# Four graph-attention layers with a planned instruction order: the planner models the port that VectorE and GpSimd share, and work moves between VectorE, GpSimd and SyncE

## The chip, the cores and the metric

The kernel runs on one core of one Trainium2 chip. The metric is the device time of one execution in microseconds (us); lower is better. The engines are called PE (TensorE matmul), PEld (its weight load), DVE (VectorE), ACT (ScalarE), POOL (GpSimd) and SP (SyncE). SP computes nothing here; it issues DMAs.

## The reference

There are 128 graphs of 128 nodes with 512 float32 features each (`x`), and one 128 x 128 integer adjacency matrix per graph (`adj`). Four layers follow each other, each a graph attention, a residual and a layer norm:

```
x = layernorm(x + gat0(x, adj))   # scores x.w_src + x.w_dst + b; leaky relu; softmax over adj + eye; mixes x itself
x = layernorm(x + gat1(adj, x))   # x @ W1 (4 heads of 256), attention, elu, then @ W2 (1024 -> 512), attention
x = layernorm(x + gat2(x, adj))   # 8 heads of 64
x = layernorm(x + gat3(x, adj))   # scores through W_fc and W_attn, mixes x itself, elu
```

Each attention is softmax(leaky_relu(s[i] + t[j]), masked by the adjacency) times a feature matrix. Graphs don't depend on each other.

## The kernel before, in words

**Tiling.** One graph is one tile: its 128 nodes are the 128 partitions, its 512 features lie along the free dimension. Everything is float32. All weights stay in SBUF; each graph's `x` is loaded once and its result stored once; the adjacency is loaded twice.

**One graph's work.** `graph(g)` builds a list of operations. Each `Op` has an engine, a cost that the planner charges, and a function that emits its instructions.

- `first` (layer 0): loads `x` (L834) and the adjacency (L835). Builds the masks: the adjacency plus the identity (`ae`, L838) and then `mask` (L738), which turns integers into 0 or a large negative number. Two dot products with the score weights (`score`, L744). Then spread, attention, mixing, residual and norm.
- `spread`: puts a column of scores into a row on all partitions. VectorE transposes the column (L589), one DMA writes it to a row in DRAM (L592), and a second reads it back broadcast over 128 partitions (L596).
- `attend`: `prelu` on ACT (L646), the masked sum with its row extreme on VectorE (L654), `exp` on ACT (L663), the reciprocal on VectorE (L671), for two of the attentions a scaling on POOL (L673), then `turned`.
- `turned`: transposes a tile. VectorE transposes 32 x 32 blocks (L607), one DMA writes them to scratch DRAM (L612), and a second reads them back with the blocks in their new places (L617 or L622).
- `project` (L710, copies out L717) multiplies by W1 or by layer 2's weights; `mixed` (L725) and `heads` (L938) multiply attention by features; `block` (L896) does so for layer 1. `halves` (L794) multiplies by W2 for two graphs together with fewer products, for which POOL forms sums and differences of the operands (L780).
- `norm`: statistics (L681, L682) on VectorE, the root on ACT (L685, L686), the `offset` (L692, and L696 in layer 2) and the scaling on ACT (L699).
- `third` (layers 2 and 3): loads the adjacency again (L975), and ends with elu (L981, L982), a sum on POOL (L986), the norm and the store (L988).

**The order.** Nothing is ordered by hand. `Pipeline.plan` places one graph's operations in a repeating period of `PERIOD` us, each engine taken by one operation at a time; from these times come the events of all graphs and the number of slots of each buffer. `Pipeline.order` then walks through the events of all 128 graphs: among those no further than `AHEAD` us past the oldest one not yet issued, it issues what could start first, by its own modelled clock of each engine, of the DMA lane and of the buffers. It uses `FLOW` for the time from one operation to a reader. `SEED` and `SPREAD` set a random shift in `plan`'s priorities. What it yields is each engine's fixed instruction order; on the chip each engine runs its own order strictly, and semaphores hold it where data or a buffer isn't ready. The modelled times are not enforced.

The weights and their derived columns are prepared by the operations of the list `setup`, which carry times of their own, up to about 200 us into the plan. POOL has four weight loads and 33 operations there.

Of the kernel before, what the change touches and what calls it, by code (L numbers as in the profile page):

```python
# [14 lines left out]
ALU = mybir.AluOpType  # L15
# [14 lines left out]

PERIOD = 28.0
LATENCY = {"PE": (0.0, 0.8), "DVE": (0.15, 1.44), "ACT": (0.1, 1.44), "POOL": (0.1, 1.44), "SP": (7.06, 7.06)}
FLOW = {"PE": (0.0, 0.6), "DVE": (0.15, 0.8), "ACT": (0.1, 0.8), "POOL": (0.1, 0.8), "SP": (4.5, 4.5)}
AHEAD = 20.0
URGENCY = 0.6
BANKS = 8

SEED, SPREAD = 989, 8.0

# [21 lines left out]
class Op:  # L61
    def __init__(self, engine, cost, emit, ins, outs, extra, uses=(), dma=0.0):
        self.dma = dma
        self.engine, self.cost, self.emit, self.extra = engine, cost, emit, extra
        self.wait = 0
        self.ins, self.outs = ins, outs
        self.uses = list(uses)
        self.bufs = list(dict.fromkeys([*ins, *outs, *uses]))

    def done(self, reader=None):  # L70
        own, other = LATENCY[self.engine]
        return self.cost + self.extra + (own if reader is self.engine else other)


class Pipeline:
# [3 lines left out]
    def plan(self, ops):  # L79
# [23 lines left out]
        taken = {e: [] for e in LATENCY}  # L103
        times, ready, missing = [0.0] * len(ops), [0.0] * len(ops), [len(q) for q in before]
# [3 lines left out]
        while waiting:  # L108
            k = min(waiting, key=lambda k: (ready[k] - URGENCY * left[k] + shift[k], k))
            waiting.remove(k)  # L110
            op, t = ops[k], ready[k]
            spans = taken[op.engine]
            while True:
                u = t % PERIOD
                clash = [
                    y + d - u for x, y in spans for d in (-PERIOD, 0.0, PERIOD)
                    if u < y + d - 1e-9 and x + d < u + op.cost - 1e-9
                ]
                if not clash:
                    break  # L120
                t += min(clash) + 1e-9
                assert t < ready[k] + 2 * PERIOD, "the period is too short"
            spans.append((t % PERIOD, t % PERIOD + op.cost))
            times[k] = t
# [20 lines left out]
    def order(self, events):  # L145

        ops, n = [e[3] for e in events], len(events)
# [33 lines left out]
        known = {e: [i for i in range(n) if not before[i] and ops[i].engine == e] for e in FLOW}  # L181
        issued, low, out = [False] * n, 0, []

        def start(i):
            t = max(clock[ops[i].engine], ready[i])
            for b in makes[i]:

                rank = 0
                for q in coming[b.tag]:
                    if q >= i or rank >= len(free[b.tag]):  # L190
                        break
                    rank += 1
                if rank >= len(free[b.tag]):
                    return None
                t = max(t, free[b.tag][rank][0])
            return t

        while len(out) < n:
# [21 lines left out]
            clock[op.engine] = done = t + op.cost  # L220
            own, other = FLOW[op.engine]
            if op.engine == "POOL":
                other += op.extra
            if op.dma:

                done = lane = max(lane, done) + op.dma
                own = other = FLOW["SP"][0]
            for q in after[i]:
# [15 lines left out]
def tile_gat_stack(  # L244
# [322 lines left out]
    def graph(g):  # L567

        ops = []

        def op(engine, cost, emit, ins=(), outs=(), extra=0.0, uses=(), dma=0.0):
            ops.append(Op(engine, cost, emit, list(ins), list(outs), extra, uses, dma))

# [5 lines left out]

        def spread(col, nh):  # L580

# [3 lines left out]
            def turn():  # L585
# [5 lines left out]
            op("DVE", 0.12 + 0.033 * nh, turn, [col.buf], [sT])  # L591
            op("SP", 0.6, lambda: nc.sync.dma_start(  # L592
                out=row.ap.rearrange("h (b c) -> b h c", b=P // 32), in_=sT.ap[0:P:32]
            ), [sT], [row], dma=0.02 + 0.03 * nh)
            db = Buf(f"db{nh}", [P, nh, P])
            op("SP", 0.4, lambda: nc.sync.dma_start(  # L596
                out=db.ap.rearrange("p h j -> p (h j)"),
# [4 lines left out]
        def turned(src, n, moving=False):  # L602
# [8 lines left out]
            ), [src], [zb])  # L611
            op("SP", 0.4, lambda: nc.sync.dma_start(  # L612
                out=scr.ap, in_=zb.ap.rearrange("p b h c -> p (b h c)")
            ), [zb], [scr], 0.2 * n, dma=0.05 + 0.17 * n)
            flat = lambda: scr.ap.rearrange("p f -> (p f)")
            if moving:
                op("SP", 0.6, lambda: nc.sync.dma_start(  # L617
                    out=out.ap.rearrange("p h i -> p (h i)").rearrange("p (q e) -> p q e", q=4),
                    in_=flat().rearrange("(q p e) -> p q e", q=4, p=P),
                ), [scr], [out], 1.0, dma=0.27 + 0.15 * n)  # L620
                return out
            op("SP", 0.65, lambda: nc.sync.dma_start(  # L622
                out=out.ap.rearrange("p h (q c) -> p h q c", q=4),
# [13 lines left out]
        def attend(db, h0, nh, src, mask, scaled=False):  # L637
# [30 lines left out]
            op("ACT", 0.08 + 0.293 * nh, prelu, [db, src.buf], [z])  # L668
            op("DVE", 0.08 + 0.225 * nh, masked, [z, mask], [zz, nm])
            op("ACT", 0.39 * nh, exp, [zz, nm], [zz, rs])  # L670
            op("DVE", 0.07, lambda: nc.vector.reciprocal(ri.ap, rs.ap), [rs], [ri])  # L671
            if scaled:
                op("POOL", 0.15 + 0.29 * nh, lambda: nc.gpsimd.tensor_mul(  # L673
                    zz.ap, zz.ap, ri.ap.unsqueeze(2).to_broadcast([P, nh, P])
                ), [zz, ri], [zz])
            return turned(zz, nh, moving=scaled), ri

        def norm(y, plus=0.0):
# [12 lines left out]
            def offset():  # L691
                nc.gpsimd.tensor_scalar(  # L692
                    out=mr.ap, in0=mv.ap[:, 0:1], scalar1=rd.ap, scalar2=-1.0, op0=ALU.mult, op1=ALU.mult
                )
                if plus:
                    nc.gpsimd.tensor_scalar_add(mr.ap, mr.ap, plus)  # L696

            op("POOL", 0.6 if plus else 0.3, offset, [mv, rd], [mr])
            op("ACT", 0.7, lambda: nc.scalar.activation(  # L699
# [37 lines left out]
        def mask(m, a, what):  # L737
            op("POOL", 0.75, lambda: nc.gpsimd.tensor_scalar(  # L738
                out=m.ap, in0=a.ap, scalar1=0.0, scalar2=-BIG, op0=what, op1=ALU.mult
            ), [a], [m], 2.0)  # L740

        def score(xv, wv, init, sc, s):
# [3 lines left out]
                accum_out=sc.ap[:, s : s + 1],  # L746
            ), [xv], [jk, sc], uses=[*w0b, b0b])

# [115 lines left out]
        def second(g, st, xl):  # L864
# [15 lines left out]
            for nh in range(2):  # L880
                op("POOL", 1.3, lambda nh=nh: nc.gpsimd.tensor_add(  # L881
                    xl.ap[:, nh, : 2 * FH], xl.ap[:, nh, : 2 * FH], b1t[:, nh * 2 * FH : (nh + 1) * 2 * FH]
                ), [xl], [xl], uses=[b1b])
# [27 lines left out]
        def third(g, st, xl2):  # L911

            m1, m2, xb = (st[n] for n in ("m1", "m2", "xb"))
            sc2 = small("sc2", 2)
            op("DVE", 0.07, lambda: nc.vector.tensor_add(sc2.ap, xl2.ap[:, :, F // 2], shift2.ap), [xl2], [sc2], uses=[shift2])
            db = spread(Col(sc2, 0, 1), 1)
# [43 lines left out]

            op("DVE", 0.2, scores, [z3, xl3], [sc4])
            mv, rd = norm(x3, plus=1.0)
# [7 lines left out]

            op("DVE", 0.15, normed, [sc4, mv, rd], [sc4], uses=[swf])
# [79 lines left out]
```

## Time and profile before

| what | us |
|---|---|
| median of 3 runs | 3219.89 (3217.49 to 3227.5) |
| the profiled execution's own time | 3260.22 |
| its span, first to last instruction | 3258.4 |
| PE busy | 3066.8 |
| VectorE busy | 2779.0 |
| ACT busy | 2451.2 |
| POOL busy | 1895.1 |

How to read it: busy time is that of the profiled execution, and the share of the span alone does not say what bounds a stage. Time in which an instruction waits for a port counts as busy; time in which it waits for a semaphore counts as idle. DMA-issuing instructions on SP don't count as busy. `A <- B` after a wait names who waited and what released it. The granted PE clock is 0.976 on average: 1.00 in the steady part, less in the first 150 and the last 150 us.

### The profile page before, as it was taken

What the parts mean: (1) busy time and instruction counts of PE and PEld (TensorE: products, weight loads), DVE (VectorE), ACT (ScalarE), POOL (GpSimd) and SP (SyncE); (2) the same over time, 40 slices, a digit from 0 to 9 for tenths busy, and PEclk for the clock granted to TensorE, in tenths of its full rate; (3) what the DMA queues carried; (4) which work ended last, traced back from release to release, by engine and by line L of the source; (5) the groups of instructions that cost most, each with busy time, mean ns of one, the idle gap of its engine ahead of it and who ended that gap; (6) DMA issues with size and microseconds to landing.
All of it is one profiled execution on the core that took longest, in us unless ns stands there. A gap on an engine that the chain in (4) does not pass through costs nothing. (4 is left out here: it accounts for less than half of the span.)

```text
span 3258.4 us, 62058 instructions
## 1 busy us (share of the span) xinstructions
PE 3066.8 (94%) x14822; PEld 2488.7 (76%) x14822; DVE 2779.0 (85%) x9833; ACT 2451.2 (75%) x8741; POOL 1895.1 (58%) x2347
## 2 busy tenths in 40 slices
PE   6899999999999999999999999999999999999984
PEld 4688887787777877877777778777787777878853
DVE  4779888888888988898888889889898898989875
ACT  2457787787777777787777877777877777778875
POOL 4655655665565655665555665565566556565533
PEclk7899999999999999999999999999999999999985
DMA  4358777877877877877778777877787787777875
GB/s 119 94 136 196 183 205 188 200 193 190 203 187 188 205 186 192 201 190 200 188 187 200 191 188 204 189 190 201 191 204 187 188 205 188 196 196 190 197 174 129
DMA packets 1657567, 606.08 MB, mean 186 GB/s; under 512 B 1311562, under 2 KB 1508170, under 8 KB 1657204
## 3 DMA queue, kind: packets, MB, share of 16 engines
q1 hardware_dynamic: 1655836, 598.97, 75.0%
q8 instruction: 120, 1.97, 0.2%
q14 instruction: 243, 1.99, 0.2%
q0 software_dynamic: 576, 2.10, 0.2%
q10 hardware_dynamic: 792, 1.06, 0.1%
HBM read 374.43 MB, written 227.48 MB: 185 GB/s over the span
## 5 line engine op out<-in xcount | busy, mean ns | idle before, releaser
L710 PE MATMUL ps<-w1s,w 128*128 128x258 f32 x4096 | 926.9, 384 | 48.5 <-DMA w<-scr 25.0
L710 PEld LDWEIGHTS ps<-w1s,w 128*128 128x128 f32 x4096 | 777.0, 191 | 186.3 <-DVE xl L812 39.5
L654 DVE CUSTOM_DVE_ANT_0 w<-w,w 128x128 f32<-128x128 f32 x1920 | 861.1, 544 | 65.6 <-ACT w L646 49.2
L794 PE MATMUL ps<-w2s,w 128*128 128x257 f32 x3584 | 849.0, 383 | 8.5 <-POOL w L780 8.4
L663 ACT ACTIVATE w<-w,nm 128x128 f32<-128x128 f32 x1920 | 748.0, 394 | 98.2 <-DVE nm L654 76.3
L794 PEld LDWEIGHTS ps<-w2s,w 128*128 128x128 f32 x3584 | 669.1, 191 | 188.8 <-issue 80.0
L646 ACT ACTIVATE w<-w,xl 128x128 f32<-128x128 f32 x1536 | 488.8, 389 | 279.9 <-DMA w<-row 259.1
L607 DVE STREAM_TRANSPOSE w<-w 128x512 f32<-128x512 f32 (+1 forms) x1024 | 551.5, 540 | 34.3 <-ACT w L663 13.3
L710 PE MATMUL ps<-wha,w 128*128 128x273 f32 x2048 | 502.3, 398 | 7.3 <-DMA w<-scr 6.9
L710 PEld LDWEIGHTS ps<-wha,w 128*128 128x128 f32 x2048 | 383.2, 192 | 87.4 <-DVE w L607 6.3
L699 ACT ACTIVATE w<-w,mr,rd 128x512 f32<-128x512 f32 x512 | 415.2, 811 | 33.9 <-POOL mr L692 33.0
L692 POOL TENSOR_SCALAR mr<-mv,rd 128x1 f32<-128x1 f32 x512 | 160.1, 313 | 409.4 <-ACT rd L686 201.8
L663 ACT ACTIVATION_READ_ACCUMULATOR w<-w,nm 128x1 f32 x1920 | 368.1, 192 | 0.0
L681 DVE BATCH_NORM_STATS2 st<-w 128x6 f32<-128x512 f32 x512 | 337.2, 668 | 5.4 <-POOL w L986 4.6
L881 POOL TENSOR_TENSOR xl<-xl,b1t 128x512 f32<-128x512 f32 x256 | 335.2, 1310 | 1.6
L938 PEld LDWEIGHTS ps<-xl,w 128*128 128x128 f32 x2048 | 274.3, 196 | 80.8 <-issue 24.4
L646 ACT ACTIVATE w<-w,sc 128x128 f32<-128x128 f32 x384 | 152.3, 397 | 227.6 <-DMA w<-row 226.6
L725 PE MATMUL ps<-w,w 128*128 128x512 f32 x512 | 277.4, 624 | 32.6 <-DMA w<-scr 31.6
L738 POOL TENSOR_SCALAR w<-adj 128x128 f32<-128x128 int32 x256 | 192.4, 752 | 188.2 <-DMA adj<-in_adj_dram 75.1
L717 ACT COPY xl<-ps 128x258 f32<-128x258 f32 (+1 forms) x768 | 273.2, 362 | 31.8 <-PE ps L710 31.3
L938 PE MATMUL ps<-xl,w 128*128 128x66 f32 x2048 | 265.2, 273 | 27.7 <-DMA w<-scr 14.4
L654 DVE DVE_READ_ACCUMULATOR2_ANT nm<- 128x1 f32 x1920 | 290.5, 151 | 0.0
(213 smaller groups left out, 4258.8 us busy)
## 6 DMA issues: line engine op xcount, KB each, us to landing
scr<-w SPq DMA_DIRECT2D x640, 256.0 KB
w<-scr SPq DMA_DIRECT2D x640, 256.0 KB
w<-row SPq DMA_DIRECT2D x128, 512.0 KB
w<-in_x_dram SPq DMA_DIRECT2D x128, 256.0 KB
w<-row SPq DMA_DIRECT2D x128, 256.0 KB
out_dram<-w SPq DMA_DIRECT2D x128, 256.0 KB
w<-row SPq DMA_DIRECT2D x384, 64.0 KB
scr<-w SPq DMA_DIRECT2D x384, 64.0 KB
```

Of the source, the lines that this page charges most:

```text
L607: op("DVE", 0.12 + 0.133 * n, lambda: nc.vector.transpose(zb.ap.rearrange("p b h c -> p h b c"), src.ap.rearrange("p (h b c) -> p h b c", ...
L646: nc.scalar.activation(z.ap[:, h, :], db.ap[:, h0 + h, :], AF.Prelu, bias=src(h0 + h), alpha=SLOPE)
L654: nc.vector.tensor_tensor_reduce(out=zz.ap[:, h, :].rearrange("p (b a) -> p a b", b=4), in0=z.ap[:, h, :].rearrange("p (a b) -> p a b", b= ...
L663: nc.scalar.activation(zz.ap[:, h, :], zz.ap[:, h, :], AF.Exp, bias=nm.ap[:, h : h + 1], scale=-1.0, accum_out=rs.ap[:, h : h + 1],)
L681: op("DVE", 0.6, lambda: nc.vector.bn_stats(st.ap, y.ap), [y], [st])
L699: op("ACT", 0.7, lambda: nc.scalar.activation(y.ap, y.ap, AF.Identity, bias=mr.ap, scale=rd.ap), [y, rd, mr], [y])
L710: op("PE", w * 4 / 2400 + 0.006, lambda k=k: nc.tensor.matmul(px.ap[:, :w], lhsT=lhs.ap[:, k, :], rhs=wa(k, c), start=(k == 0), stop=(k == ...
L717: op("ACT", 0.06 + w / 1200, lambda: nc.scalar.copy(dst(), px.ap[:, :w]), [px], [t])
L725: op("PE", width * 4 / 2400, lambda: nc.tensor.matmul(pa.ap[:, :width] if len(xv.shape) == 2 else pa.ap.rearrange("p (s c) -> p s c", s=2) ...
L794: return lambda: nc.tensor.matmul(q[b].ap[:, :C2], lhsT=x()[:, k, :], rhs=w2s[:, slot, k, :], start=(fresh and k == 0), stop=(k == 3), ski ...
L881: op("POOL", 1.3, lambda nh=nh: nc.gpsimd.tensor_add(xl.ap[:, nh, : 2 * FH], xl.ap[:, nh, : 2 * FH], b1t[:, nh * 2 * FH : (nh + 1) * 2 * F ...
L938: op("PE", 0.225, lambda u=u, h=h: nc.tensor.matmul(pa.ap[:, u * CH : (u + 1) * CH], lhsT=pt.ap[:, u, :], rhs=xl3.ap[:, h * CH : (h + 1) * ...
```

## The change

The change has five parts. Lines past L568 stand 14 further down after it.

1. The planner has a notion of the port that VectorE and GpSimd share: an `Op` with `port` set may not overlap another such operation, in `plan` and in `order`. All POOL arithmetic has it, and on VectorE the masked sum, `score`, `ae`, `sc2`, `scores` and `normed`.
2. `order` holds a DMA of SP back until the eighth DMA before it has landed (`WINDOW`, `LANDING`), and counts DMAs by their own latency whoever issues them.
3. The constants differ: period, latencies, look-ahead, seed, and the costs of many operations, such as 2.0 us for one of the reads of `turned`.
4. Masks, `ae` and offsets go from POOL to VectorE.
5. The loads of `x` and of the adjacency, the store, and layer 0's two DMAs of `spread` go from SP's queue to POOL's.

The computation is the same. Cut to its core:

```diff
-PERIOD = 28.0
-LATENCY = {"PE": (0.0, 0.8), "DVE": (0.15, 1.44), "ACT": (0.1, 1.44), "POOL": (0.1, 1.44), "SP": (7.06, 7.06)}
-FLOW = {"PE": (0.0, 0.6), "DVE": (0.15, 0.8), "ACT": (0.1, 0.8), "POOL": (0.1, 0.8), "SP": (4.5, 4.5)}
-AHEAD = 20.0
+PERIOD = 32.0
+LATENCY = {"PE": (0.0, 0.8), "DVE": (0.15, 1.88), "ACT": (0.1, 1.88), "POOL": (0.1, 1.88), "SP": (7.44, 7.44)}
+FLOW = {"PE": (0.0, 0.6), "DVE": (0.15, 0.8), "ACT": (0.1, 0.8), "POOL": (0.1, 0.8), "SP": (3.2, 3.2)}
+AHEAD = 45.0
+WINDOW, LANDING = 8, 2.0
-SEED, SPREAD = 989, 8.0
+SEED, SPREAD = 433, 8.0
...
+        self.port = port or (engine == "POOL" and not dma)
...
-        own, other = LATENCY[self.engine]
+        own, other = LATENCY["SP" if self.dma else self.engine]
...
-                    y + d - u for x, y in spans for d in (-PERIOD, 0.0, PERIOD)
+                    y + d - u for x, y in (spans + ports if op.port else spans) for d in (-PERIOD, 0.0, PERIOD)
...
+            if ops[i].engine == "SP" and len(landed) >= WINDOW:
+                t = max(t, landed[-WINDOW])
+            if ops[i].port:
+                t = max(t, port)
...
-            op("SP", 0.4, lambda: nc.sync.dma_start(
+            op(by, 0.52 if by == "SP" else 0.9, lambda: queue[by].dma_start(
...
-                nc.gpsimd.tensor_scalar(
+                nc.vector.tensor_scalar(
                     out=mr.ap, in0=mv.ap[:, 0:1], scalar1=rd.ap, scalar2=-1.0, op0=ALU.mult, op1=ALU.mult
                 )
...
-            op("POOL", 0.6 if plus else 0.3, offset, [mv, rd], [mr])
+            op("DVE", 0.14 if plus else 0.08, offset, [mv, rd], [mr])
...
-            op("POOL", 0.75, lambda: nc.gpsimd.tensor_scalar(
+            op("DVE", 0.2, lambda: nc.vector.tensor_scalar(
                 out=m.ap, in0=a.ap, scalar1=0.0, scalar2=-BIG, op0=what, op1=ALU.mult
-            ), [a], [m], 2.0)
+            ), [a], [m])
...
-            op("SP", 0.4, lambda: nc.sync.dma_start(out=x0.ap, in_=x[g]), [], [x0], 1.0, dma=0.72)
-            op("SP", 0.4, lambda: nc.sync.dma_start(out=at.ap, in_=adj[g]), [], [at], 1.0, dma=0.22)
+            op("POOL", 0.9, lambda: nc.gpsimd.dma_start(out=x0.ap, in_=x[g]), [], [x0], 1.0, dma=0.72)
+            op("POOL", 0.9, lambda: nc.gpsimd.dma_start(out=at.ap, in_=adj[g]), [], [at], 1.0, dma=0.22)
...
-            op("POOL", 0.6, lambda: nc.gpsimd.tensor_tensor(out=ae.ap, in0=at.ap, in1=eye_i, op=ALU.add), [at], [ae])
+            op("DVE", 0.2, lambda: nc.vector.tensor_tensor(out=ae.ap, in0=at.ap, in1=eye_i, op=ALU.add), [at], [ae], port=True)
...
-            db = spread(Col(sc0, 1, 1), 1)
+            db = spread(Col(sc0, 1, 1), 1, "POOL")
...
-            op("SP", 0.4, lambda: nc.sync.dma_start(out=at.ap, in_=adj[g]), [z3], [at], 1.0, dma=0.22)
+            op("POOL", 0.9, lambda: nc.gpsimd.dma_start(out=at.ap, in_=adj[g]), [z3], [at], 1.0, dma=0.22)
...
-            op("SP", 0.4, lambda: nc.sync.dma_start(out=out[g], in_=y.ap), [y], [], 1.0, dma=0.72)
+            op("POOL", 0.9, lambda: nc.gpsimd.dma_start(out=out[g], in_=y.ap), [y], [], 1.0, dma=0.72)
```

More of the change, by code (lines that the diff above doesn't have):

```diff
@@ L61, with __init__ @@
 class Op:
-    def __init__(self, engine, cost, emit, ins, outs, extra, uses=(), dma=0.0):
+    def __init__(self, engine, cost, emit, ins, outs, extra, uses=(), dma=0.0, port=False):
         self.dma = dma
+        self.port = port or (engine == "POOL" and not dma)
         self.engine, self.cost, self.emit, self.extra = engine, cost, emit, extra
@@ L102, in plan @@
             )
-        taken = {e: [] for e in LATENCY}
+        taken, ports = {e: [] for e in LATENCY}, []
         times, ready, missing = [0.0] * len(ops), [0.0] * len(ops), [len(q) for q in before]
@@ L121, in plan @@
                 t += min(clash) + 1e-9
-                assert t < ready[k] + 2 * PERIOD, "the period is too short"
+                assert t < ready[k] + 3 * PERIOD, "the period is too short"
             spans.append((t % PERIOD, t % PERIOD + op.cost))
+            if op.port:
+                ports.append(spans[-1])
             times[k] = t
@@ L181, in order @@
         known = {e: [i for i in range(n) if not before[i] and ops[i].engine == e] for e in FLOW}
-        issued, low, out = [False] * n, 0, []
+        issued, low, out, landed, port = [False] * n, 0, [], [], 0.0
         def start(i):
             t = max(clock[ops[i].engine], ready[i])
+            if ops[i].engine == "SP" and len(landed) >= WINDOW:
+                t = max(t, landed[-WINDOW])
+            if ops[i].port:
+                t = max(t, port)
             for b in makes[i]:
@@ L220, in order @@
             clock[op.engine] = done = t + op.cost
+            if op.port:
+                port = done
             own, other = FLOW[op.engine]
-            if op.engine == "POOL":
-                other += op.extra
             if op.dma:
@@ L227, in order @@
                 own = other = FLOW["SP"][0]
+                if op.engine == "SP":
+                    landed.append(done + LANDING)
+            elif op.engine == "POOL":
+                other += op.extra
             for q in after[i]:
@@ L569, in graph, with op @@
         ops = []
-        def op(engine, cost, emit, ins=(), outs=(), extra=0.0, uses=(), dma=0.0):
-            ops.append(Op(engine, cost, emit, list(ins), list(outs), extra, uses, dma))
+        def op(engine, cost, emit, ins=(), outs=(), extra=0.0, uses=(), dma=0.0, port=False):
+            ops.append(Op(engine, cost, emit, list(ins), list(outs), extra, uses, dma, port))
         def bank():
@@ L578, in small, with spread @@
             return Buf(tag, [P, n])
-        def spread(col, nh):
+        def spread(col, nh, by="SP"):
             sT, row = Buf(f"sT{nh}", [P, nh, 32]), Buf(f"row{nh}", [nh, P])
@@ L591, in spread @@
             op("DVE", 0.12 + 0.033 * nh, turn, [col.buf], [sT])
-            op("SP", 0.6, lambda: nc.sync.dma_start(
+            op(by, 0.64 if by == "SP" else 0.9, lambda: queue[by].dma_start(
                 out=row.ap.rearrange("h (b c) -> b h c", b=P // 32), in_=sT.ap[0:P:32]
@@ L611, in turned @@
             ), [src], [zb])
-            op("SP", 0.4, lambda: nc.sync.dma_start(
+            op("SP", 0.52, lambda: nc.sync.dma_start(
                 out=scr.ap, in_=zb.ap.rearrange("p b h c -> p (b h c)")
@@ L616, in turned @@
             if moving:
-                op("SP", 0.6, lambda: nc.sync.dma_start(
+                op("SP", 0.52, lambda: nc.sync.dma_start(
                     out=out.ap.rearrange("p h i -> p (h i)").rearrange("p (q e) -> p q e", q=4),
@@ L621, in turned @@
                 return out
-            op("SP", 0.65, lambda: nc.sync.dma_start(
+            op("SP", 2.0 if n == 4 else 0.75, lambda: nc.sync.dma_start(
                 out=out.ap.rearrange("p h (q c) -> p h q c", q=4),
@@ L668, in attend @@
             op("ACT", 0.08 + 0.293 * nh, prelu, [db, src.buf], [z])
-            op("DVE", 0.08 + 0.225 * nh, masked, [z, mask], [zz, nm])
+            op("DVE", 0.08 + 0.225 * nh, masked, [z, mask], [zz, nm], port=True)
             op("ACT", 0.39 * nh, exp, [zz, nm], [zz, rs])
@@ L672, in attend @@
             if scaled:
-                op("POOL", 0.15 + 0.29 * nh, lambda: nc.gpsimd.tensor_mul(
+                op("POOL", 0.15 + 0.22 * nh, lambda: nc.gpsimd.tensor_mul(
                     zz.ap, zz.ap, ri.ap.unsqueeze(2).to_broadcast([P, nh, P])
@@ L695, in offset @@
                 if plus:
-                    nc.gpsimd.tensor_scalar_add(mr.ap, mr.ap, plus)
-            op("POOL", 0.6 if plus else 0.3, offset, [mv, rd], [mr])
+                    nc.vector.tensor_scalar_add(mr.ap, mr.ap, plus)
+            op("DVE", 0.14 if plus else 0.08, offset, [mv, rd], [mr])
             op("ACT", 0.7, lambda: nc.scalar.activation(
@@ L746, in score @@
                 accum_out=sc.ap[:, s : s + 1],
-            ), [xv], [jk, sc], uses=[*w0b, b0b])
+            ), [xv], [jk, sc], uses=[*w0b, b0b], port=True)
         def halves(hT):
@@ L880, in second @@
             for nh in range(2):
-                op("POOL", 1.3, lambda nh=nh: nc.gpsimd.tensor_add(
+                op("POOL", 1.36, lambda nh=nh: nc.gpsimd.tensor_add(
                     xl.ap[:, nh, : 2 * FH], xl.ap[:, nh, : 2 * FH], b1t[:, nh * 2 * FH : (nh + 1) * 2 * FH]
@@ L914, in third @@
             sc2 = small("sc2", 2)
-            op("DVE", 0.07, lambda: nc.vector.tensor_add(sc2.ap, xl2.ap[:, :, F // 2], shift2.ap), [xl2], [sc2], uses=[shift2])
+            op("DVE", 0.07, lambda: nc.vector.tensor_add(sc2.ap, xl2.ap[:, :, F // 2], shift2.ap), [xl2], [sc2], uses=[shift2], port=True)
             db = spread(Col(sc2, 0, 1), 1)
@@ L959, in scores @@
                 nc.vector.tensor_add(sc4.ap, sc4.ap, xl3.ap[:, C3 - 2 :])
-            op("DVE", 0.2, scores, [z3, xl3], [sc4])
+            op("DVE", 0.25, scores, [z3, xl3], [sc4], port=True)
             mv, rd = norm(x3, plus=1.0)
@@ L969, in normed @@
                 nc.vector.tensor_scalar_mul(sc4.ap, sc4.ap, rd.ap)
-            op("DVE", 0.15, normed, [sc4, mv, rd], [sc4], uses=[swf])
+            op("DVE", 0.15, normed, [sc4, mv, rd], [sc4], uses=[swf], port=True)
             at, m3 = Buf("adj", [P, P], I32), Buf("m3", [P, P])
-            op("SP", 0.4, lambda: nc.sync.dma_start(out=at.ap, in_=adj[g]), [z3], [at], 1.0, dma=0.22)
+            op("POOL", 0.9, lambda: nc.gpsimd.dma_start(out=at.ap, in_=adj[g]), [z3], [at], 1.0, dma=0.22)
             mask(m3, at, ALU.is_equal)
```

## The prediction

> **What bounds the kernel now.** I read the page's busy times first, then a steady stretch by window, then what the matmul engine waits for there, then the VectorE groups. Lines are named by their numbers before the change.
>
> ```profile
> PE 3066.8 (94%) x14822; PEld 2488.7 (76%) x14822; DVE 2779.0 (85%) x9833; ACT 2451.2 (75%) x8741; POOL 1895.1 (58%) x2347
> 300.00:3000.00 2700.00, 2609.49 (x12856) 2135.26 (x12855) 2376.62 (x8493) 2115.03 (x7597) 1613.76 (x2008) 1.00 0.79 194
> ```
>
> The first line is the whole span, the second 300 to 3000 us: busy PE, PEld, DVE, ACT, POOL, then clock, DMA share, GB/s. That stretch holds 445 POOL offsets (L692), four to a graph, so 111.25 graphs and 2700 / 111.25 = 24.27 us a graph. PE is busy 2609.49 / 111.25 = 23.46 us of it, DVE 21.36, ACT 19.01, POOL 14.51. PE bounds the kernel, at full clock. Its idle is 90.5 us there; the whole span has 3258.4 - 3066.8 = 191.6, so 101 lie in the filling and emptying. Waits of PE in the steady stretch (total us, times, longest):
>
> ```profile
> PE ps L710 <- DMA w<-scr: 25.0, 24, 2.1
> PE ps L725 <- DMA w<-scr: 15.2, 27, 1.3
> PE ps L850 <- DVE w L903: 15.0, 15, 1.9
> PE ps L710 <- DVE ri L671: 9.3, 9, 2.1
> PE ps L710 <- DVE st L681: 8.4, 5, 2.0
> ```
>
> 40.2 of the 90.5 us end with a transposed tile coming back from DRAM. The rest is mostly VectorE being late. In the first 200 us one more wait is named:
>
> ```profile
> PE ps L850 <- POOL w L738: 12.6, 2, 9.0
> ```
>
> POOL builds the masks there, in a queue with the weight products. VectorE carries a loss of its own. From the groups kept apart by shape (busy us, mean ns):
>
> ```profile
> L654 DVE CUSTOM_DVE_ANT_0 w<-w,w 128x128 f32<-128x128 f32 x1920 | 861.1, 544 | 65.6 <-ACT w L646 49.2 <-DMA row<-w 11.2 <-ACT w L663 3.8
> L959 DVE TENSOR_TENSOR sc<-sc,xl 128x2 f32<-128x2 f32 x128 | 81.6, 638 | 4.4
> L956 DVE TENSOR_REDUCE sc<-z 128x2 f32<-128x16 f32 x128 | 21.9, 171 | 0.1
> L692 POOL TENSOR_SCALAR mr<-mv,rd 128x1 f32<-128x1 f32 x512 | 160.1, 313 | 409.4 <-ACT rd L686 201.8 <-DVE nm L654 128.2 <-DVE st L681 19.2
> L318 POOL DMA_DIRECT2D w2s<-in_L_gnn_W_dram x4 | 3.2, 809 | 0.1
> ```
>
> and from the timelines of DVE and POOL at 1502 us (start, length):
>
> ```profile
> 1502.56 1.16 DVE L654 CUSTOM_DVE_ANT_0 w<-w,w 128x128 f32<-128x128 f32 x1
> 1503.57 0.39 DVE L654 CUSTOM_DVE_ANT_0 w<-w,w 128x128 f32<-128x128 f32 x1
> 1502.43 1.04 POOL L673 TENSOR_TENSOR w<-w,ri 128x512 f32<-128x512 f32 x1
> ```
>
> The same masked sum takes 0.39 us, or 1.16 where a POOL operation began just before it: it ends about when POOL lets go. The mean of 544 against 390 is 0.15 us on each of 15 a graph, 2.3 us; L959, two columns wide, loses 638 - 171 = 0.47 us. So some 2.8 of VectorE's 21.36 us a graph are waits for POOL that count as busy.
>
> **The Trainium skill.** "SBUF — State Buffer", section "Who interferes with whom", says that a VectorE instruction with two SBUF inputs contends with a GpSimd instruction that reads SBUF, and that whichever starts first holds the shared port throughout. The trace agrees: 1.16 against 0.39 us. Section "SBUF: two separate sides" warns that a DMA issued from GpSimd can be starved of descriptors while VectorE holds both ports; no row here shows it. "DMA: Bandwidth & Descriptors", section "Issuing engines are not separate DMA queues", says that DMAs of all issuers share the same 16 engines and another issuer saves only sequencer time. Here those engines stand at 0.79 in the steady stretch, and I expect that share to stay.
>
> **The change part by part, per graph.** (1) POOL loses three masks (L738: 192.4 + 106.0 us over the run), the diagonal sum (L838: 58.8), four offsets and one plus (L692, L696: 160.1 + 33.2): 550.5 / 128 = 4.30 us. (2) POOL gains six DMA issues: x, adjacency twice, the output, and the two of layer 0's spread. At 0.81 us from L318 that is 4.9 us. Bounds: 0.4 each, as SP's cheapest issues take (L835 median 408 ns), to 1.6, double for descriptor starvation: 2.4 to 9.7. POOL ends at 14.51 - 4.30 + 4.9 = 15.1, or 12.6 to 19.9, below 24.27 in any case. Its order is strict, though: layer 0's second spread DMA waits for the first to land, the output store for ACT's L699, and behind them stand the sums L780 for which PE's L794 waits. In the written order those sums lead their matmuls by 7.0 us of PE work before and 7.7 after (positions in the printed order, the matmuls between priced by their rows). One such wait of up to 4 us is covered; two together are not. (3) SP loses those six issues, medians 0.45 + 0.41 + 0.45 + 0.39 + 0.54 + 0.42 = 2.7 of some 14.7 us. SP bounds nothing, but the other 24 issues queue behind less. (4) VectorE gains nine small instructions. Low: masks and sum at 0.2 us (the step between neighbours of L607's 128x128 transposes in the timeline), offsets at 0.07: 1.15. High: four at 0.29 (L607's mean there), the sum 0.15 more for the port, five at 0.27 (L969's mean): 2.66. I take 1.5, being small unlinked instructions that overlap in the timeline. Against it, POOL time that can hold the port falls by 4.30 of 14.51, 30%, which frees 0.3 x 2.8 = 0.8 us; that the order now keeps port users apart frees 0 to 1.4 more, taken as 0.4, since nothing but the modelled times enforces it. VectorE: 21.36 + 1.5 - 1.2 = 21.7 (20.3 to 23.2), still under PE's 23.46.
>
> (5) The order itself. From the printed orders of both programs, graphs 30 to 100, mean PE work between a DMA's issue and its reader: transposed tile to the mixing matmul L725, 2.9 before and 11.1 after; to L938, 6.1 and 11.0; broadcast row to L646 on ACT, 4.2 and 8.2; x to L744, 2.8 and 12.1; the shortest tenth for L710, 4.4 and 9.2. Every DMA stands further ahead of its reader. But from VectorE's transpose, not the DMA, to the reader, the distances hardly grow: L725 16.8 to 20.9, L938 19.3 to 19.0, L646 17.6 to 15.8. The gain is real where SP was late, none where the data was. So of the 40.2 us of waits for tiles I let 30 go; of the other 50, 10, for a VectorE that is no slower and a mask that no longer queues on POOL. What is late next is VectorE's output (L671, L681, L903). (6) Filling: the 12.6 us of masks go; the loads of x now stand on POOL beside four weight loads (3.2 us) and 33 setup operations, which gives some 3 back: 10. Emptying: 17 graphs in flight instead of 16 by the order; after the last graph's last layer-2 projections 12.1 us of PE work are left instead of 13.1, so nothing.
>
> Sum: 30 + 10 + 10 = 50 us off the profiled execution's own 3260.22 (span 3258.4), so 3210, 0.985 of it. The median of the runs shown, 3219.89, lies 1.2% lower than that execution; the same share gives 3170.
>
> **Rivals.** **No gain:** the transposes are no earlier against their readers, so only L725's 15 us and some of the filling go, and VectorE's lateness takes them back. For it: the end-to-end distances of (5), and SP, which often stands waiting for VectorE (L592 for L671, 135.9 us). Against: L725 and x do gain lead. 0 to 20 us: 3200 to 3222, at 3213. **Slower, VectorE becomes the bound:** its additions cost the high 2.66 us and the port gives nothing back. Then it needs 24.0 us a graph, more than PE's 23.46. It decides from 2.1 us net. Even half-way, at 23.2, VectorE has 1.1 us of slack in a graph instead of 2.9 and passes its waits on; I price 0.3 to 0.6 us a graph, times 128: 40 to 75 us, so 3258 to 3294, at 3265. For it: 88% busy already and nine more instructions in strict order. Against: the port time it gets back. **The order does not hold on the chip:** port users collide as before, since no semaphore parts them; then L654's mean stays near 510, and this leads to one of the two cases above.
>
> **How the numbers follow.** About 0.3% is what a measurement of this kernel can tell from no change: under 3210 is faster, over 3230 slower. Likeliest, 0.58: 3170, own range 3125 to 3205. No gain, 0.19, of which a third falls under 3210. Slower, 0.23. That makes faster 0.64, same 0.12, slower 0.24. The lower end: if all waits for tiles and half of the others go, 40 + 25 + 15 = 80 us, 3141, and somewhat better matmul packing takes it to 3125. The upper end reaches into the slower case, to 3262.
>
> **What would show it.** Right: PE idle in 300 to 3000 us near 50 us with L725's and L710's waits for w<-scr under 15 together; L654's mean under 500 ns; L692's and L738's rows on DVE at about 0.1 and 0.2 us; POOL's DMA rows near 0.8 us; no wait of PE on a mask in the filling. Wrong: DVE over 23 us a graph; L794 waiting for L780 by tens of us, which is the POOL queue; waits of L744 or the masks for x or the adjacency over 100 us; or a steady graph that still takes 24.2 us.

## The result and the profile after: VectorE is the bound

The changed kernel takes 3357.05 us (median of 4 runs, 3355.36 to 3359.06) against 3223.1 us for the kernel before (4 runs): a ratio of 1.0417, 95% interval 1.0397 to 1.0437. The forecast was 3170 us and faster; it is 134 us slower. The kernel before was measured anew beside each set of experiments, and its median there lay between 3239 and 3261 us, so the experiments are given as ratios. The profiled execution of before, 3260.22 us, lies at the upper end of that; that of the changed kernel is 3356.74 us. The two traces therefore show 96.6 us of span (3355.0 - 3258.4) and not the whole 134.

From the changed kernel's page, busy time of each engine over the span; then, from its windows, the stretch from 300 to 3000 us (us, and busy PE, PEld, DVE, ACT, POOL, then clock, DMA share, GB/s):

```profile
PE 3105.1 (93%) x14822; PEld 2506.0 (75%) x14822; DVE 3184.2 (95%) x10985; ACT 2453.6 (73%) x8741; POOL 1778.0 (53%) x1963
300.00:3000.00 2700.00, 2580.03 (x12561) 2102.18 (x12561) 2653.97 (x9260) 2070.28 (x7413) 1475.04 (x1631) 0.99 0.80 189
```

VectorE is busy for 2653.97 of 2700 us, 98.3%, where it was 88.0%. By the 433 batch statistics (L695) in that stretch, four to a graph, 108.25 graphs pass: 24.94 us a graph instead of 24.27, of which VectorE needs 24.52 us and PE 23.83. PE's idle time there went up from 90.5 to 120.0 us. PE's own busy time rose by 0.37 us a graph, from 23.46, at clock 0.99 instead of 1.00; why is not shown. The page's chain of waits, which before put 1% of the span on VectorE, 1% on ACT and 0% on the rest, now runs through the kernel, and on VectorE:

```profile
DVE 54%; ACT 13%; issue 12%; PE 10%; DMA 10%; POOL 1%; SPq 1%; DVEq 0%; ACTq 0%; POOLq 0%
```

What PE waits for in the same stretch (total us, times, longest), first the largest, then all that are left for transposed tiles. L724 and L739 are L710 and L725 of before, which had 40.2 us; L952 is L938:

```profile
PE ps L739 <- ACT xl L731: 41.7, 30, 2.2
PE ps L724 <- DVE xl L826: 16.4, 21, 0.9
PE ps L724 <- DVE w L917: 12.1, 12, 1.1
...
PE ps L952 <- DMA w<-scr: 2.2, 3, 1.0
...
PE ps L739 <- DMA w<-scr: 0.7, 1, 0.7
```

The waits for tiles are as good as gone, as forecast; those for VectorE and ACT stand in their place. ACT itself waits for VectorE: its largest wait in that stretch is 359.2 us for the batch statistics, L699 on L696. VectorE's own waits there, the largest:

```profile
DVE ri L685 <- ACT w L677: 10.4, 27, 0.8
```

It never stands still for long. And these are the groups of VectorE and POOL that the prediction spoke of (busy us, mean ns, then idle before):

```profile
L668 DVE CUSTOM_DVE_ANT_0 w<-w,w 128x128 f32<-128x128 f32 x1920 | 874.7, 557 | 5.1 <-ACT w L660 4.6 <-ACT rd L699 0.2
L973 DVE TENSOR_TENSOR sc<-sc,xl 128x2 f32<-128x2 f32 x128 | 171.3, 1338 | 4.4
L752 DVE TENSOR_SCALAR w<-adj 128x128 f32<-128x128 int32 x256 | 103.7, 405 | 2.3 <-DMA adj<-in_adj_dram 1.9 <-DMA scr<-w 0.4
L706 DVE TENSOR_SCALAR mr<-mv,rd 128x1 f32<-128x1 f32 x512 | 96.0, 199 | 11.4 <-ACT rd L700 11.4
L752 DVE TENSOR_SCALAR w<-ae 128x128 f32<-128x128 int32 x128 | 34.2, 267 | 0.2
L710 DVE TENSOR_SCALAR mr<-mr 128x1 f32<-128x1 f32 x128 | 19.7, 154 | 4.4
L852 DVE CUSTOM_DVE_ANT_0 ae<-adj,eye_i 128x256 uint16<-128x256 uint16 x128 | 56.1, 439 | 3.3 <-DMA adj<-in_adj_dram 3.3
L610 POOL DMA_DIRECT2D w<-row x128 | 72.3, 565 | 49.9 <-ACT w L677 17.1 <-DVE w L752 11.2 <-DMA row<-sT 6.9
```

The masked sum L668 (L654 before) did not fall from 544 ns but rose to 557, and the two-column addition L973 (L959) doubled, from 638 to 1338 ns. POOL does 30% less arithmetic, and VectorE waits more for it.

**How much is waiting for the port.** I took, for each VectorE instruction that can contend, its length in the stretch from 300 to 3000 us less the length that it has where no POOL operation overlaps it, counted where it was longer: 380 ns for the masked sum, 695 for the dot products, 160, 137, 210 and 229 for the small score operations, 212 for a mask, 279 for the diagonal sum. Per graph that is 3.3 us before and 5.6 after. The terms: the masked sum 2.5 to 2.8, L973 0.5 to 1.2, the dot products 0.2 to 0.5, the other score operations 0.2 to 0.6, the new masks and the diagonal sum 0 to 0.4. These are lengths; where two instructions overlap while they wait, both are counted.

### The profile page after: what moved, and what is told of

It reads as the page before. It is cut to its first block, busy times and chain, and to the rows that moved or that the text cites. A ratio compares the mean times of both kernels' runs of the same rounds, so it can differ in the third digit from the quotient of the medians.

```text
span 3355.0 us, 62374 instructions
## 1 busy us (share of the span) xinstructions
PE 3105.1 (93%) x14822; PEld 2506.0 (75%) x14822; DVE 3184.2 (95%) x10985; ACT 2453.6 (73%) x8741; POOL 1778.0 (53%) x1963
## 3 DMA queue, kind: packets, MB, share of 16 engines
q10 hardware_dynamic: 792, 1.06, 0.1%
## 4 chain that ended last, share of the span: by engine, by line
DVE 54%; ACT 13%; issue 12%; PE 10%; DMA 10%; POOL 1%; SPq 1%; DVEq 0%; ACTq 0%; POOLq 0%
DVE w L668 13%; DVE w L621 8%; ACT w L677 6%; DVE st L695 6%; PE ps L724 5%; DMA w<-scr 4%; DVE w L747 4%; DMA scr<-w 3%; PE ps L808 2%; DVE w L758 2%; DVE w L917 2%; DMA w<-row 2%; ACT w L713 2%; DVE sT L603 2%; DVE w L752 2%
## 5 line engine op out<-in xcount | busy, mean ns | idle before, releaser
L724 PE MATMUL ps<-w1s,w 128*128 128x258 f32 x4096 | 934.5, 384 | 29.0 <-DVE xl L826 16.4
L724 PEld LDWEIGHTS ps<-w1s,w 128*128 128x128 f32 x4096 | 779.8, 191 | 170.3 <-DVE xl L826 25.6
L668 DVE CUSTOM_DVE_ANT_0 w<-w,w 128x128 f32<-128x128 f32 x1920 | 874.7, 557 | 5.1 <-ACT w L660 4.6
L808 PE MATMUL ps<-w2s,w 128*128 128x257 f32 x3584 | 862.6, 384 | 13.8 <-POOL w L794 12.2
L621 DVE STREAM_TRANSPOSE w<-w 128x512 f32<-128x512 f32 (+1 forms) x1024 | 550.7, 541 | 24.3 <-ACT w L677 14.3
L724 PE MATMUL ps<-wha,w 128*128 128x273 f32 x2048 | 524.3, 408 | 38.9 <-DVE w L917 12.1
L724 PEld LDWEIGHTS ps<-wha,w 128*128 128x128 f32 x2048 | 390.5, 196 | 176.3 <-ACT xl L731 40.0
L699 ACT ACTIVATE rd<-mv,eps 128x1 f32<-128x1 f32 x512 | 150.8, 294 | 414.6 <-DVE mv L696 411.0
L687 POOL TENSOR_TENSOR w<-w,ri 128x512 f32<-128x512 f32 (+1 forms) x256 | 196.8, 769 | 417.6 <-DVE ri L685 292.3
L695 DVE BATCH_NORM_STATS2 st<-w 128x6 f32<-128x512 f32 x512 | 341.9, 672 | 6.4 <-POOL w L1000 6.2
L739 PE MATMUL ps<-w,w 128*128 128x512 f32 x512 | 285.4, 641 | 53.1 <-DMA w<-scr 34.5
L895 POOL TENSOR_TENSOR xl<-xl,b1t 128x512 f32<-128x512 f32 x256 | 322.7, 1276 | 0.8
L952 PEld LDWEIGHTS ps<-xl,w 128*128 128x128 f32 x2048 | 270.3, 195 | 60.4 <-ACT xl L731 15.8
L952 PE MATMUL ps<-xl,w 128*128 128x66 f32 x2048 | 263.9, 273 | 31.6 <-DMA w<-scr 20.9
L668 DVE DVE_READ_ACCUMULATOR2_ANT nm<- 128x1 f32 x1920 | 288.1, 150 | 0.0
L794 POOL TENSOR_TENSOR w<-w,w 128x512 f32<-128x512 f32 x192 | 246.6, 1287 | 63.0 <-ACT w L677 21.6
```

The lines of the kernel that those rows point to most:

```text
L621: op("DVE", 0.12 + 0.133 * n, lambda: nc.vector.transpose(zb.ap.rearrange("p b h c -> p h b c"), src.ap.rearrange("p (h b c) -> p h b c", ...
L668: nc.vector.tensor_tensor_reduce(out=zz.ap[:, h, :].rearrange("p (b a) -> p a b", b=4), in0=z.ap[:, h, :].rearrange("p (a b) -> p a b", b= ...
L695: op("DVE", 0.6, lambda: nc.vector.bn_stats(st.ap, y.ap), [y], [st])
L724: op("PE", w * 4 / 2400 + 0.006, lambda k=k: nc.tensor.matmul(px.ap[:, :w], lhsT=lhs.ap[:, k, :], rhs=wa(k, c), start=(k == 0), stop=(k == ...
L739: op("PE", width * 4 / 2400, lambda: nc.tensor.matmul(pa.ap[:, :width] if len(xv.shape) == 2 else pa.ap.rearrange("p (s c) -> p s c", s=2) ...
L808: return lambda: nc.tensor.matmul(q[b].ap[:, :C2], lhsT=x()[:, k, :], rhs=w2s[:, slot, k, :], start=(fresh and k == 0), stop=(k == 3), ski ...
```

## The experiments

All moved operations can be emitted on either engine with the order left as it is, since an order that holds for all engines together is valid whichever engine runs an operation. Most runs use that. "Small" means the masks, the diagonal sum and the offsets; "DMAs" the six that moved. The measured columns are the ratio to the kernel before with its interval, VectorE's busy share of the stretch from 300 to 3000 us, and the waits for the port per graph, worked out as above. The changed kernel was measured in one set only. Where an experiment is compared with it, two sets are compared, and the median of before alone differs by up to 1.2% between sets (3223 to 3261 us).

| order | small on | DMAs on | ratio | DVE | port us |
|---|---|---|---|---|---|
| before | POOL | SP | 1 | 88.0% | 3.3 |
| changed | DVE | POOL | 1.0417 (1.0397 to 1.0437) | 98.3% | 5.6 |
| changed | POOL | SP | 1.0037 (1.0020 to 1.0054) | 88.5% | 3.2 |
| before | DVE | POOL | 1.0449 (1.0431 to 1.0466) | 98.7% | 6.0 |
| changed | POOL | POOL | 0.9893 (0.9877 to 0.9909) | 94.7% | 4.6 |
| changed | DVE | SP | 1.0113 (1.0094 to 1.0131) | 96.7% | 4.6 |
| changed | DVE | ACT | 1.0077 (1.0057 to 1.0097) | 96.0% | 4.4 |
| before | POOL | POOL | 0.9864 (0.9840 to 0.9888) | 94.8% | 4.9 |
| before | POOL | POOL, spread on SP | 0.9799 (0.9783 to 0.9815) | 96.6% | 5.0 |
| before | POOL | ACT | 0.9642 (0.9628 to 0.9657) | 92.5% | 3.6 |

**1. Is it the order?** The changed order with all operations on their old engines:

```diff
-                nc.vector.tensor_scalar(
+                nc.gpsimd.tensor_scalar(
                     out=mr.ap, in0=mv.ap[:, 0:1], scalar1=rd.ap, scalar2=-1.0, op0=ALU.mult, op1=ALU.mult
...
-            op("POOL", 0.9, lambda: nc.gpsimd.dma_start(out=x0.ap, in_=x[g]), [], [x0], 1.0, dma=0.72)
+            op("POOL", 0.9, lambda: nc.sync.dma_start(out=x0.ap, in_=x[g]), [], [x0], 1.0, dma=0.72)
```

and the same for the masks, the sum, the other loads, the store and the spread.

> The changed kernel's planner and order, but every moved operation is emitted on its old engine: masks, diagonal sum and offsets on GpSimd, all DMAs on SyncE. Theory V (VectorE has become the bound, by the nine instructions added to it and by longer waits for the port): VectorE falls from 24.5 to about 21.5 us a graph and the time to 3180 to 3250 us. Theory O (the new order itself is the worse one): stays at 3320 us or above. Theory D (the DMAs on GpSimd's queue cost it): also about 3220 us, so D is told from V by the next runs.

3250.69 us against 3238.67: 1.0037. The other way round, the old order with the new engines:

> The kernel before with its own planner and order, but with all moved operations emitted on their new engines. Theory V: VectorE carries the nine instructions, about 23.5 to 24.5 us a graph, 3290 to 3370 us. Theory O: about 3220 us. Theory D: 3290 us or above too.

3384.28 us, 1.0449, with VectorE at 98.7%. So the order is neither the harm nor a gain worth speaking of: what the operations run on decides, in both orders alike. Theory O falls.

**2. Small operations or DMAs?** From the changed kernel, one of the two moves undone at a time.

> The changed kernel with masks, diagonal sum and offsets emitted on GpSimd again; the DMAs stay on GpSimd's queue and the order stays the new one. Theory V: VectorE at 21 to 22 us a graph and 3190 to 3260 us, with GpSimd at some 17 us. Theory D: still 3320 us or above, since GpSimd's queue is fuller than ever. Theory O: 3320 us or above.

3202.99 us, 0.9893: faster than both kernels.

> The changed kernel with the loads, the store and layer 0's spread emitted on SyncE again; masks and offsets stay on VectorE. Theory V: VectorE stays at 24 us a graph or more and the time at 3320 to 3360 us; a little lower if the DMA issues on GpSimd lengthen the holds of the port. Theory D: falls to 3220 to 3260 us. Theory O: stays at 3350 us.

3272.03 us, 1.0113, with VectorE at 96.7%. Here theory V missed: it had put this run at 3320 to 3360 us and the other within reach of the kernel before. The two moves do not add. The six DMAs on POOL are worth 1.4% where the small operations are on POOL (1.0037 to 0.9893), and cost 3.0% where they are on VectorE (1.0113 to 1.0417; 2.6% by the times themselves).

**3. The waits for the port themselves.** The changed kernel without two POOL additions a graph (it leaves out b1); VectorE's instructions are the same.

```diff
-                op("POOL", 1.36, lambda nh=nh: nc.gpsimd.tensor_add(
-                    xl.ap[:, nh, : 2 * FH], xl.ap[:, nh, : 2 * FH], b1t[:, nh * 2 * FH : (nh + 1) * 2 * FH]
-                ), [xl], [xl], uses=[b1b])
+                op("POOL", 1.36, lambda: None, [xl], [xl], uses=[b1b])
```

> The changed kernel without layer 1's bias additions on GpSimd (two instructions of 1.28 us a graph); it leaves out that b1 is added, and nothing else. VectorE's instructions and the order are the same. Theory P (the ports: what VectorE waits for GpSimd's reads is a large part of its new load): GpSimd's reading falls from 10.5 to 7.9 us a graph, VectorE's waits for the port from 5.6 to some 4 us, and the time by 100 us or more. Theory C (the count of the nine added instructions alone is the cause): VectorE loses nothing that binds, and the time falls by less than 40 us.

3225.94 us, 0.9895 against the changed kernel's 1.0417: 5.0% less (3.9% by the times themselves), for two instructions on an engine that was busy for 55% of the stretch. The waits fell to 4.0 us a graph, from 5.6, as theory P had it, and VectorE's busy time from 24.52 to 22.84. The stretch in this run:

```profile
300.00:3000.00 2700.00, 2649.72 (x13110) 2182.93 (x13109) 2598.09 (x9670) 2167.66 (x7743) 1252.96 (x1472) 1.00 0.83 198
```

The count of the added instructions alone, theory C, would not have moved the time. The run also takes 2.6 us a graph out of POOL's queue; but the bound is VectorE, and its busy time fell by 1.7 us with the same instructions. The other side of it, half of the small operations put back:

> The changed kernel with the three masks and the diagonal sum on GpSimd again, the offsets still on VectorE, the DMAs on GpSimd's queue. Theory V (VectorE's load decides): VectorE loses about 1.5 us a graph, of 24.5; GpSimd gains 2.8. Some 3210 to 3260 us. If the offsets are what hurts: above 3320 us.

3295.85 us, 1.0110 (1.0084 to 1.0136).

> The changed kernel with the four offsets and the plus on GpSimd again, masks and diagonal sum on VectorE, the DMAs on GpSimd's queue. Theory V: VectorE loses about 0.9 us a graph, so less is gained than with the masks: 3260 to 3320 us. If the masks, which also wait for the port, cost nothing: about 3200 us.

3301.10 us, 1.0129 (1.0099 to 1.0159). The first lies above its range, the second within. As ratios each half gives back 3 of the 5 points, their intervals overlap, and which is the heavier can't be told. VectorE is still at 96.8% and 98.1% in them.

**4. Why the same DMAs help or hurt.** In the old order, with nothing else changed:

> The kernel before with its own order; only the six DMAs a graph are emitted on GpSimd's queue. If the DMAs on GpSimd are a gain by themselves, as between the two runs with the new order and the small operations on GpSimd (3251 and 3203 us), 3170 to 3220 us. If their gain needs the new order, which lets loads be issued well ahead of their readers, 3240 us or above: the old order puts the adjacency load 2.2 us of matmul work ahead of its mask, and GpSimd's queue would stand still behind its waits.

3216.25 us, 0.9864. The gain needs no new order. The waits of PE for transposed tiles, 40.2 us before, do not appear in this run's stretch at all; the largest there are

```profile
PE ps L850 <- DVE w L903: 20.6, 14, 1.7
PE ps L794 <- POOL w L780: 16.1, 32, 0.8
```

and yet VectorE's waits for the port rise from 3.3 to 4.9 us a graph with the same arithmetic on POOL. The changed kernel's trace shows two ways. POOL first, then VectorE, at 1040 us (start, length):

```profile
1040.45 0.57 POOL L610 DMA_DIRECT2D w<-row  x1
1041.04 1.28 POOL L794 TENSOR_TENSOR w<-w,w 128x512 f32<-128x512 f32 x1
1042.27 1.28 POOL L1000 TENSOR_TENSOR w<-w,w 128x512 f32<-128x512 f32 x1
1040.61 2.96 DVE L980 SCALAR_TENSOR_TENSOR sc<-swf,mv,sc 128x2 f32<-128x2 f32 x1
```

A two-column operation that takes 0.21 us alone begins while POOL issues a DMA and no POOL arithmetic runs, and it doesn't get through before the two operations behind the DMA have ended.

The first way is the early start. Over the stretch, 68 masked sums began during a DMA issue that a POOL operation followed within 60 ns: 1.59 us on average, though 19 of them took under 0.4. Where POOL's next operation came later, 139 took 0.37 us on average. And 107 that began with POOL idle, 0.2 to 0.6 us ahead of a POOL operation, took 0.38 on average, none over 0.40. So the DMA issue itself holds nothing, but an operation queued close behind it mostly does so early.

The second is the length of the hold. Take a row of POOL instructions, each beginning within 60 ns of the end of the one ahead. With no DMA in front, VectorE gets in after the first operation. So it is with the same two, L794 and L1000, in the run of the changed order with the DMAs on SP:

```profile
347.45 1.28 POOL L794 TENSOR_TENSOR w<-w,w 128x512 f32<-128x512 f32 x1 [2.97 <-PE ps L952]
348.68 1.33 POOL L1000 TENSOR_TENSOR w<-w,w 128x512 f32<-128x512 f32 x1
347.62 1.34 DVE L668 CUSTOM_DVE_ANT_0 w<-w,w 128x128 f32<-128x128 f32 x1
```

With a DMA in front it mostly waits for the whole row. In the changed kernel:

```profile
1050.00 0.54 POOL L989 DMA_DIRECT2D adj<-in_adj_dram  x1
1050.55 1.19 POOL L964 TENSOR_TENSOR w<-z,w 128x512 f32<-128x512 f32 x1
1051.69 1.27 POOL L895 TENSOR_TENSOR xl<-xl,b1t 128x512 f32<-128x512 f32 x1
1052.91 1.27 POOL L876 TENSOR_TENSOR w<-w,b2t 128x512 f32<-128x512 f32 x1
1054.14 1.26 POOL L895 TENSOR_TENSOR xl<-xl,b1t 128x512 f32<-128x512 f32 x1
1050.21 5.43 DVE L668 CUSTOM_DVE_ANT_0 w<-w,w 128x128 f32<-128x128 f32 x1
```

I counted the masked sums, dot products and two-column operations that began during a POOL operation with another right behind it, and waited. With no DMA in front, all 101 in the changed kernel got in after the first operation, and all 103 in the run with the DMAs on SP. With a DMA in front, 77 of 78 waited through two. Over all runs, 7 of 2815 waited through two or more without a DMA in front, and 580 of 730 with one. Waits that begin in a row with a DMA in front are 2.8 of the changed kernel's 5.6 us: 1.2 begin during the issue, 1.6 later.

Two tests on ACT's queue:

```diff
-            op("POOL", 0.9, lambda: nc.gpsimd.dma_start(out=x0.ap, in_=x[g]), [], [x0], 1.0, dma=0.72)
+            op("POOL", 0.9, lambda: nc.scalar.dma_start(out=x0.ap, in_=x[g]), [], [x0], 1.0, dma=0.72)
```

and so for the five others.

> The changed kernel with the six DMAs a graph emitted on ACT's queue instead of GpSimd's; masks and offsets stay on VectorE. Theory H (a DMA issue on GpSimd right ahead of a GpSimd operation lengthens the hold of the port, and that is why the same DMAs cost 3% where VectorE is the bound): no wait for the port begins with a DMA, VectorE waits 4.4 to 4.8 us a graph instead of 5.6, and the time is 0.99 to 1.02 of the kernel before. Theory Q (SyncE's relief and the landing of the DMAs matter, not the port): as with GpSimd's queue, 1.04. A rival on ACT itself: its strict order stands behind the DMAs' waits, ACT's idle time before PRELU rises, and the time goes over 1.03.

3273.01 us, 1.0077. No wait begins with a DMA, since POOL's queue has none in this stretch, and the waits fall to 4.4 us. Theory H holds, theory Q falls: off POOL's queue, the DMAs take back 3.4 of 4.2 points even with the small operations on VectorE.

> The kernel before with its own order; the six DMAs a graph are emitted on ACT's queue. If the gain of 1.4% on GpSimd's queue is SyncE's relief, ACT's queue gives it too, less what six issues cost ACT (some 2.4 us of 24, with ACT at 19): 0.985 to 1.0. If it depends on GpSimd's own DMA rings: 1.0 or above. If ACT's strict order stands behind the store's and the spread's waits: above 1.01.

3133.74 us, 0.9642: the best version, 3.6% faster than the kernel before, and better than was expected of it. Its stretch:

```profile
300.00:3000.00 2700.00, 2692.44 (x13443) 2242.50 (x13444) 2496.51 (x8881) 2234.83 (x7958) 1674.44 (x2089) 1.00 0.83 203
```

PE is busy for 99.7%, and its waits for transposed tiles, whose DMAs stay on SP, are down to 3.8 us. VectorE's waits for the port are 3.6 us a graph, against 4.9 with the six on POOL. ACT's 19.0 us a graph left room for six issues.

> The kernel before with its own order; only the two adjacency loads, the load of x and the store go to GpSimd's queue, layer 0's spread stays on SyncE. If SyncE's relief is what the DMAs on GpSimd bring, four of six issues bring most of it: 0.985 to 0.993 of the kernel before. If it is layer 0's spread, a chain of two DMAs with a wait between them: 0.995 to 1.0.

3185.22 us, 0.9799: better than all six on POOL, and than this run's expectation. Layer 0's spread on POOL takes away more than it gives; why, beside the wait for its first DMA to land, was not tried.

What these runs take off SP: its DMA-issuing instructions lasted 21.0 us of 24.3 us a graph before, 87% of the time, and last 16.2 with the six on POOL and 16.4 with them on ACT.

**5. Does the modelled port hold on the chip?** The changed planner without it:

```diff
-        self.port = port or (engine == "POOL" and not dma)
+        self.port = False
```

> The changed kernel with the planner's knowledge of the port switched off: operations of VectorE and GpSimd may overlap in plan and order as before; engines, queues and all other constants as changed. It gives another order, so 0.5% either way is no sign of anything. If the modelled port keeps collisions away on the chip: VectorE's waits rise from 5.6 to 7 us a graph or more and the time to 1.06 or more of the kernel before. If modelled times don't hold on the chip, which only the semaphores bind: waits of 5 to 6 us and 1.035 to 1.05.

3317.21 us, 1.0209, with 5.3 us of waits for the port. Faster than either theory had it. That the order that knows the port is the slower of the two is not settled: 3317.21 and 3357.05 us come from two sets and differ by 1.2%, no more than the medians of before do. But its waits, 5.6 us, are not fewer, so modelling the port did not keep the collisions away here. One order against one other says no more than that.

## Why the prediction was wrong, point by point

**What bounds the kernel before.** PE, right in the main. But SP at 87% and VectorE at 88% stood close behind it, and I took only VectorE for a danger.

**Step (4), VectorE's load: the step that failed.** It forecast +0.3 us a graph, 1.5 for the additions less 1.2 that the port would give back. VectorE's busy time rose by 24.52 - 21.36 = 3.16.

The additions were sized right in sum. Their lengths are (103.7 + 34.2 + 56.1 + 96.0 + 19.7) / 128 = 2.42 us, but an instruction of VectorE often begins before the one ahead has ended. If each stretch of VectorE's busy time is counted once, for the instruction that carries it on, the nine take 1.5 us of a steady graph, waits of their own included. That the sum came out so close is partly luck: an offset is 199 ns and not 70, though a mask is 210 ns alone, as the low case had it, and 405 or 267 as it ran.

What failed is the return from the port, which had the wrong sign. I took 1.2 us off, because POOL's arithmetic falls by 30% and the order keeps the users apart. Counted once in the same way, VectorE's old instructions take some 1.7 us more. By lengths the waits rose by 2.2 us, from 3.3 to 5.6. In the changed order, they are 3.2 us with everything on its old engine, so that order gave 0.1 of the 0.4 that I took for it; 4.6 with the small operations on VectorE; and 5.6 with the DMAs on POOL as well. Proportion was the wrong idea. For the last step, experiment 4 shows why: a DMA in front of POOL operations makes the hold longer. Why the waits rise with the small operations alone, while POOL reads less, is only argued: a VectorE that is always running meets more of what POOL reads. That POOL's reading is what VectorE waits for is shown: 2.6 us less of it gave 1.6 us less waiting (experiment 3).

The rival **"VectorE becomes the bound"** was the right one, with the decisive point, 2.1 us, well placed. Its upper case, 24.0 us, was still below what came: it took the additions too high, and it only let the port give nothing back. That the port could take more was not in it. Its price of 3258 to 3294 us fell short for that reason, and so did the range, which ended at 3262. The rival **"the order does not hold on the chip"** was right about the collisions.

**Step (1) and (2), POOL.** Right: POOL bounds nothing, 13.6 us a graph. A DMA issue measures 0.56 to 0.59 us and not 0.81, none of the six over 0.7, so the starvation that the upper bound allowed for does not show. That such an issue lengthens the hold of the port was in no bound. L794's queue was no loss in the steady stretch: 0.2 us of PE waits.

**Step (3), SP.** "SP bounds nothing" came out of median durations, 14.7 us a graph. The means hold the tail: L617's median is 0.43 us and its mean over the run 1.06, and the sum is 21.0. Relief of SP is the part of the change that is worth something, where VectorE is not the bound: 1.4% on POOL's queue, 3.6% on ACT's. With the small operations on VectorE, ACT's queue gives no clear gain over SP's (1.0077 and 1.0113).

**Step (5), the waits for tiles.** I let 30 of 40.2 us go; 0.7 remain on these two lines. The direction was right, but I put it down to the order. The order alone, with the DMAs on SP, left 32.5 us of it and the time where it was (experiment 1); the queue made it go (experiment 4).

**Step (6), filling.** The 12.6 us of waits for a mask from POOL became 17.0 us for a mask from VectorE in the first 200 us. PE was idle for 56.4 us of the first 300 instead of 41.0. After 3000 us it was idle for 73.5 instead of 60.1, where I had put nothing.

## What to carry to other kernels

Price an operation that is moved to an engine by that engine's slack in the steady stretch, with the waits that hide inside its busy time, and allow for both signs in these waits: here they rose from 3.3 to 5.6 us while POOL's arithmetic fell by 30%. Add up busy time, not lengths, where instructions overlap. Sum the issue time of a DMA queue from means over the whole run, not from medians. And before moving DMAs off a full queue onto POOL's, try another queue: ACT's was the better here by 2.2 points. Keeping DMA issues away from rows of POOL operations would be the next thing to try; no run here did.

## What the runs showed of the hardware that I had not expected

- Successive POOL operations let VectorE in between, unless a DMA issue stands right in front of them; then it mostly has to wait on. Over all runs, 7 of 2815 waits passed two or more such operations without a DMA in front, 580 of 730 with one. L980 waited 2.96 us through two, one masked sum 5.43 us through four.
- A POOL operation queued within 60 ns of a DMA issue mostly blocks VectorE already during that issue: 1.59 against 0.37 us for a masked sum. Of the 68 cases, 62 are L794 behind L610 or L1002. The issue alone blocks nothing.
- Issuing a DMA on POOL takes 0.56 to 0.59 us for 64 KB broadcast, 256 KB or half a KB alike.
- The masks (`tensor_scalar`, one SBUF source, integer to float) also wait for POOL: 0.21 us alone, 0.75 on average where a POOL operation overlapped.
